# Converting attention weights to fp16 by DMA instead of by ScalarE, VectorE and GpSimd, and dealing VectorE's other steps one a unit

## Chip, cores, metric

The kernel runs on one core of one Trainium2 chip. The metric is the device time of one execution in microseconds (us).

## What is computed

Eight images of 512 channels and 32 x 32 = 1024 tokens go through two attention layers. The change is in the first layer:

```
h   = group_norm(x); qkv = qkv_w @ h + qkv_b          # 8 heads of 64 channels
q, k, v = fake_quant(q), fake_quant(k), fake_quant(v) # 8 bits, one scale for the whole tensor
w   = softmax(q^T k / sqrt(64)) over the keys
a   = v w^T
x   = x + proj_w @ a + proj_b
```

The second layer is group norm, single-head attention over all 512 channels, a projection and the residual, image by image.

## The kernel before

**Stages.** First, q, k and v of all images are computed and stored in DRAM with their minima and maxima, since the quantizing scales need the whole tensor. Then the first layer's attention runs for all images (`attention`, a generator). Image 0's attention runs alone, beside a weight folding for the second layer (`fold`, L208 `fold` matmuls), which one `next(folding)` per odd unit deals out to TensorE. From image 1 on, the attention of an image runs between the second-layer blocks of the image before.

**Units.** The attention's unit is (image b, pair of heads j, half hf of the queries, key tile s): 8 images x 4 pairs x 2 halves x 8 key tiles = 512 units, 64 of them in image 0. A unit does, in this order:

- `scores`: two `st` matmuls (one for each head of the pair), then ScalarE's exponential from PSUM into `pt` (128 x 1024, fp32). `pt` comes from a ring of four buffers.
- `split`: `pt` is turned into two fp16 parts, `two`: a high part (a cast) and a low part (`pt` minus the high part, a subtraction on VectorE, the inner function `rest`). `two` comes from a ring of six.
- `over_keys`: eight `av` matmuls with the quantized v (four column quarters, two parts).
- `totals`: four `sm` matmuls with ones, for the softmax's sums.

In image 0 the units with `plain(b, s)`, that is s = 3 and 7, aren't split. Their `pt` lies in a separate ring of three (`aside`), and `av` and `sm` are fp32 matmuls on it, with an fp32 copy of v (`vfs`, written by `whole`). Of image 0's other units, s = 2 and 6 are cast by GpSimd, s = 5 by VectorE, and s = 0, 1 and 4 by ScalarE.

**Order.** A step of the main loop handles four units: `st` runs six to eight units ahead of `av`; `need(u - 4)` makes sure that the subtraction of unit u - 4 has been written before the exponential of unit u. After the last unit of a pair, `finish` copies `av` and `sm` out of PSUM by ScalarE, sends the sums through DRAM to be spread (`apart`, `rs_d`, then `rs`, which comes back as a broadcast), and VectorE divides (`divide`, writing `ao`). At the first unit of a pair `load_pair` fetches the next pair's q, k and v into `raw` buffers (two of them, on SP's DMA queue), and VectorE quantizes them in two steps each (`quant`, `quant2`).

From image 1's third loop step on, the class `InOrder` plans the order on VectorE and ScalarE by hand with costs and due times (`later`, `fill`, `settle`; `InOrder.planned` is true). In image 0's attention and the first eight units of image 1 it isn't: `later` does its work at once, and the framework's scheduler orders the engines' instructions, with the written order as a priority. Nearly all of VectorE's and ScalarE's instructions carry the helper's line L91, all matmuls L208; tiles tell them apart.

Of the kernel before, what the change touches and what calls it, by code (L numbers as in the profile page):

```python
# [9 lines left out]
F32 = mybir.dt.float32  # L10
# [8 lines left out]
P = 128  # L19
# [3 lines left out]
NT = T // P  # L23
NH = T // 512
HEADS = 8
PAIRS = HEADS // 2
# [32 lines left out]
def attn_pair_kernel(  # L59
# [9 lines left out]
    nc = tc.nc  # L69
# [236 lines left out]
    with ExitStack() as fast:  # L306
# [39 lines left out]
        cut, at = {}, 0  # L346
# [526 lines left out]
        def quant2(raw, dst, i):  # L873
            dve.tensor_scalar(dst, raw, bhi[:, i : i + 1], MAGIC, ALU.min, ALU.subtract)
# [35 lines left out]
        vfs = {}  # L910

        def plain(b, s):
            return b == 0 and s % 4 == 3

        ao = {}

        def load_pair(b, j):

            nm = f"{b}_{j}"
            raws = []  # L920

# [12 lines left out]
            def whole(raw, _, i):  # L934
                quant2(raw.rearrange("p (t d) -> p t d", t=NT)[:, 3::4, :], vfs[j], i)

            fetch(0, q_d[b][j])
            fetch(1, k_d[b][j])
            qt = qkp.tile([P, T], BF, tag="q", name=f"q_{nm}")
            kt = qkp.tile([P, T], BF, tag="k", name=f"k_{nm}")  # L940
            vt = qkp.tile([P, NT, P], F16, tag="v", name=f"v_{nm}")
            todo = (qt, kt, vt.rearrange("p t d -> p (t d)"))

            if b == 0:
                vfs[j] = xp.tile([P, 2, 256], F32, tag="x", name=f"vf_{nm}")[:, :, 0:P]

            def quants(i):
                for step in (quant, quant2, *([whole] if i == 2 and b == 0 else [])):
                    dve.later(
                        "qk" if i < 2 else "qv", 0.7, lambda step=step: step(raws[i], todo[i], i),  # L950
                        pe.t + 12.0, 45.0,
                    )

            def fetch_v():
                if len(raws) == 2:
                    fetch(2, v_d[b][:, :, bass.ts(j, P)])
                quants(2)

            if (b, j) == (0, 0):
                fetch(2, v_d[b][:, :, bass.ts(j, P)])  # L960
            quants(0)
            quants(1)
            dve.later("qk", 0.0, fetch_v)
            return qt, kt, vt

        settle = dve.settle

        def attention():

# [4 lines left out]
                     for s in range(NT)]  # L974
            pairs = {}
            pairs[0, 0] = load_pair(0, 0)
            pts, parts, avs, sms, rss, ready = {}, {}, {}, {}, {}, {}
# [4 lines left out]
            def scores(u):  # L982
                b, j, hf, s = units[u]
                if hf == 0 and s == 0:
                    settle("qk")
                nm = f"{b}_{j}_{hf}"
                qt, kt, _ = pairs[b, j]
                st = pair_ps(f"st_{nm}_{s}")
                if b == 0 and u % 2 == 1:
                    next(folding, None)  # L990
                awaits(st_free[-2])
                for i, r in enumerate(HALF):
                    mm(
                        st[:, i, :], lhsT=kt[r, bass.ts(s, P)],
                        rhs=qt[r, bass.ts(hf, 512)], start=True, stop=True,
                    )
                if u >= 4:
                    need(u - 4)
                if plain(b, s):
                    pt = aside[:, u // 4 % 3].rearrange("p (i k) n -> p i (k n)", i=2)  # L1000
                else:
                    pt = ptp.tile([P, 2, 512], F32, tag="p", name=f"pt_{nm}_{s}")
                there = act.do(
                    1.12, lambda: act.activation(pt, st, AF.Exp, scale=esc),
                    max(pe.t + 0.25, ready.get(u - 4, 0.0) + 0.1),
                )
                st_free.append(there)
                pts[u] = pt, there

            def split(u):  # L1010

                b, j, hf, s = units[u]
                pt, there = pts.pop(u)
                if plain(b, s):
                    parts[u], ready[u] = pt, there
                    return
                two = partp.tile([P, 2, 2, 512], F16, tag="two", name=f"two_{b}_{j}_{hf}_{s}")
                parts[u] = two

                def rest():  # L1020
                    dve.tensor_tensor(two[:, 1], pt, two[:, 0], ALU.subtract)
                    ready[u] = dve.t

                def cast(copy=act.copy):
                    at_hand.add(u)
                    copy(two[:, 0], pt)  # L1026
                    done_at = act.t if copy == act.copy else there + 1.5
                    dve.later("sum", elements(1024), rest, done_at + 0.1, 9.0)

                if s % 4 == 2:  # L1030
                    cast(nc.gpsimd.tensor_copy)
                elif not InOrder.planned and s == 5:
                    cast(dve.tensor_copy)
                else:
                    act.later("cast", 1.02, cast, there, 7.0)

            def need(u):

                while u not in ready:
                    e, name = (act, "cast") if u not in at_hand else (dve, "sum")  # L1040
                    e.begin(next(i for i, c in enumerate(e.chores) if c[0] == name))

            def over_keys(us):
                need(us[-1])
                awaits(ready[us[-1]])
                pe.t += 0.12
                for u in us:
                    b, j, hf, s = units[u]
                    if s == 0:
                        avs[b, j, hf] = av_bank(f"av_{b}_{j}_{hf}")  # L1050
                    if plain(b, s):
                        for i in range(4):
                            r = slice(i * QUAD, (i + 1) * QUAD)
                            mm(
                                avs[b, j, hf][r, :], lhsT=vfs[j][:, s // 4, r],
                                rhs=parts[u][:, i // 2, :], start=False, stop=(s == NT - 1),
                            )
                        continue
                    for w in range(2):
                        for i in range(4):  # L1060
                            r = slice(i * QUAD, (i + 1) * QUAD)
                            mm(
                                avs[b, j, hf][r, :], lhsT=pairs[b, j][2][:, s, r],
                                rhs=parts[u][:, w, i // 2, :], start=(s == 0 and w == 0),
                                stop=(s == NT - 1 and w == 1),
                            )
# [17 lines left out]
            def finish(b, j, hf):  # L1084

                nm = f"{b}_{j}"
                if hf == 0:
# [35 lines left out]

            for u in (0, 2, 4):
                for i in (u, u + 1):
# [3 lines left out]
            for u in range(0, len(units), 4):  # L1129
                b, j, hf, s = units[u]  # L1130
                if hf == 0 and s == 0:
                    n = b * PAIRS + j + 1
                    if n < B * PAIRS:
                        pairs[divmod(n, PAIRS)] = load_pair(*divmod(n, PAIRS))
                    settle("qv")


# [28 lines left out]
                    two(split, u + 6)  # L1166
                    two(scores, u + 8)
                if s == NT - 4:
                    finish(b, j, hf)
# [993 lines left out]
```

## Time and profile before

| | |
|---|---|
| three runs, us | 2590.61, 2591.39, 2596.20 (median 2591.39) |
| the profiled execution, us | 2596.26, its span 2594.5 |
| busy share of the span | TensorE 98%, VectorE 73%, ScalarE 52%, GpSimd 7% |
| DMA | 243 MB, mean 94 GB/s |
| first `st` matmul of the attention | starts at 590.0 us |
| `aside` exponentials of image 0 | 16, the last starts at 703.1 us |
| first projection matmul of image 0 | starts at 726.0 us |

In the profile PE is TensorE's matmuls, PEld its weight loads, DVE VectorE, ACT ScalarE, POOL GpSimd, SP the queue that issues most DMAs. A group reads: line, engine, operation, output <- inputs, shapes, count | busy us, mean ns of one | idle us of the engine just before, with what released it. A busy TensorE isn't TensorE at its peak, as matmuls overlap at their ends. Two neighbouring `st` matmuls, one for each head, run beside each other.

### The profile page before, as it was taken

Reading aid. Unit: us, or ns where it says so; the run is one execution under the profiler, and the core shown is the slowest. Engines: PE = TensorE matmul, PEld = TensorE weight load, DVE = VectorE, ACT = ScalarE, POOL = GpSimd, SP = SyncE. Lnnn points to the kernel's source line nnn. Section 1 sums busy time; section 2 is a strip of 40 time slices with the busy share of each in tenths; the row PEclk is TensorE's granted clock in tenths of the full one; section 3 lists DMA queues with packets and bytes.
Section 4 is the critical chain, followed back from the end, with each engine's and each line's share of the span. In section 5 each row is a group of like instructions: output and inputs, shape, how many; then the busy total and the mean of one; then the engine's idle time right before and its main releaser. Section 6 shows DMA issues by size and latency. Waiting matters only on the chain.

```text
span 2594.5 us, 38713 instructions
## 1 busy us (share of the span) xinstructions
PE 2535.6 (98%) x15670; PEld 1754.2 (68%) x15670; DVE 1905.8 (73%) x2748; ACT 1360.4 (52%) x1696; POOL 193.8 (7%) x153
## 2 busy tenths in 40 slices
PE   7999999999989999999999999999999999999998
PEld 4788888873237765775677577757766775777687
DVE  6788777669867777777877787778777777775544
ACT  3222222218856674666566566647665765664121
POOL 0000000001110001000100011010001000100000
PEclk9899999999999999999999999999999999999999
DMA  4343333334311232223212332231232123212211
GB/s 167 130 148 139 115 119 118 129 126 135 115 50 54 58 111 102 66 78 111 87 56 70 125 99 58 94 107 63 85 107 98 46 79 122 83 51 84 86 37 38
DMA packets 156014, 243.09 MB, mean 94 GB/s; under 512 B 26545, under 2 KB 93105, under 8 KB 154289
## 3 DMA queue, kind: packets, MB, share of 16 engines
q1 hardware_dynamic: 125264, 182.81, 21.3%
q10 hardware_dynamic: 30560, 57.71, 6.5%
q8 instruction: 125, 2.05, 0.3%
q14 instruction: 65, 0.52, 0.1%
HBM read 153.64 MB, written 86.28 MB: 92 GB/s over the span
## 4 chain that ended last, share of the span: by engine, by line
PE 84%; DVE 5%; ACT 2%; issue 2%; DMA 2%; POOL 0%; SPq 0%; ACTq 0%; DVEq 0%
PE s L208 15%; PE o L208 14%; PE qkps L208 12%; PE pj L208 9%; PE av L208 7%; PE v2ps L208 7%; PE g L208 7%; PE vps L208 6%; PE st L208 4%; PE sm L208 3%; DVE two L91 2%; ACT pt L91 1%; DMA rs<-rs_d 0%; DVE acc L91 0%; DVE h L91 0%
## 5 line engine op out<-in xcount | busy, mean ns | idle before, releaser
L91 ACT ACTIVATE pt<-st,esc 128x1024 f32<-128x1024 f32 x496 | 528.6, 1115 | 348.7 <-PE st L208 326.2
L91 DVE TENSOR_TENSOR two<-pt,two 128x1024 f16<-128x1024 f32 x496 | 604.3, 1235 | 129.2 <-POOL two L1026 106.9
L91 ACT CAST two<-pt 128x1024 f16<-128x1024 f32 x358 | 362.6, 1056 | 5.3 <-ACT p L91 5.1
L1026 POOL CAST two<-pt 128x1024 f16<-128x1024 f32 x128 | 171.3, 1338 | 1537.3 <-ACT pt L91 771.5
L208 PE MATMUL av<-two,v 128*32 128x512 f16 x3968 | 244.7, 381 | 0.2
L208 PE MATMUL s<-g,h 128*128 128x256 f32 x1024 | 233.4, 380 | 0.0
L208 PE MATMUL pj<-ao,wp 128*128 128x512 f32 x512 | 223.8, 595 | 0.0
L208 PEld LDWEIGHTS s<-g,h 128*128 128x128 f32 x1024 | 192.9, 190 | 31.0 <-issue 4.3
L91 ACT ACTIVATE u_ring<-qkps,qkbt 128x512 f32<-128x512 f32 x89 | 61.1, 687 | 252.6 <-PE qkps L208 220.3
L208 PE MATMUL st<-q,k 64*128 64x512 bf16 x1024 | 165.8, 383 | 17.6 <-ACT pt L91 12.6
L208 PEld LDWEIGHTS <-v 128*32 128x32 f16 x3968 | 91.3, 96 | 134.0 <-issue 60.7
L208 PE MATMUL s<-g,sums 128*128 128x256 f32 x768 | 178.4, 381 | 0.2 <-DVE p L91 0.2
L208 PEld LDWEIGHTS pj<-ao,wp 128*128 128x128 f32 x512 | 96.0, 190 | 121.6 <-issue 111.1
L208 PE MATMUL o<-p,v 128*128 128x256 f32 x768 | 175.2, 382 | 1.0 <-DVE p L91 1.0
L208 PEld LDWEIGHTS o<-p,v 128*128 128x128 f32 x768 | 144.3, 190 | 27.1 <-issue 5.7
L208 PEld LDWEIGHTS s<-g,sums 128*128 128x128 f32 x768 | 144.7, 190 | 24.2 <-issue 4.1
L208 PEld LDWEIGHTS <-k 64*128 64x128 bf16 x1024 | 35.6, 94 | 156.6 <-issue 155.0
L208 PE MATMUL sm<-two,ones 128*32 128x512 f16 x1984 | 136.1, 379 | 1.9 <-ACT rs L91 1.9
L208 PE MATMUL qkps<-half,w_high 128*128 128x512 f32 x480 | 134.3, 402 | 0.0
L208 PE MATMUL qkps<-half,w_low 128*128 128x512 f32 x480 | 132.3, 398 | 1.9 <-DVE half L91 1.9
L208 PE MATMUL qkps<-half,w_mix 128*128 128x512 f32 x480 | 132.5, 398 | 0.6 <-DVE half L91 0.6
L208 PE MATMUL g<-h,wa 128*128 128x256 f32 x512 | 122.0, 387 | 2.7 <-DVE h L91 2.5
(219 smaller groups left out, 3838.3 us busy)
## 6 DMA issues: line engine op xcount, KB each, us to landing
rs<-rs_d SPq DMA_DIRECT2D x80, 256.0 KB
x<-in_x_dram SPq DMA_DIRECT2D x32, 512.0 KB
q_d<-wa SPq DMA_DIRECT2D x32, 512.0 KB
k_d<-wa SPq DMA_DIRECT2D x32, 512.0 KB
v_d<-v_ring SPq DMA_DIRECT2D x32, 512.0 KB
raw<-q_d SPq DMA_DIRECT2D x32, 512.0 KB
raw<-k_d SPq DMA_DIRECT2D x32, 512.0 KB
x_d<-h SPq DMA_DIRECT2D x64, 256.0 KB
```

Source lines behind the costliest of these rows:

```text
L91: ins = self.latest = op(*args, **kw).ins
L208: ins = nc.tensor.matmul(ps, lhsT=lhsT, rhs=rhs, **kw).ins
L1026: copy(two[:, 0], pt)
```

## The change

Image 0 keeps one fp32 unit in eight (s = 7). Of the other seven, s = 1, 2, 3, 5 and 6 get their high part by a casting DMA, `pt` (fp32) to `two` (fp16) in SBUF, issued from GpSimd's queue; s = 0 and 4 stay on ScalarE. The subtraction of a unit cast by DMA is put off: it is written when the unit two later is split, or when `need` asks for it. The branch by which VectorE casts s = 5 while nothing is planned is deleted, so in image 1's first units ScalarE casts that tile.

VectorE's other steps of the unplanned part (quantizing, the fetch of v, the reciprocal `spread`, `divide`) go into a list, `dealt`, each with the unit from which it may run: 10 units after the load for q, k and the fetch of v, 18 for v, 10 after `finish` for `spread` and 15 for `divide`. Each `split` then writes one of them at most; `settle(what)` writes all that are left of a kind where the program needs them.

```diff
         def plain(b, s):
-            return b == 0 and s % 4 == 3
+            return b == 0 and s % 8 == 7
+        dealt = []
+        def deal(u):
+            i = next((i for i, (at, *_) in enumerate(dealt) if at <= u), None)
+            if i is not None:
+                dealt.pop(i)[2]()
+        def settle(what):
+            while True:
+                i = next((i for i, (_, name, _) in enumerate(dealt) if name == what), None)
+                if i is None:
+                    break
+                dealt.pop(i)[2]()
+            dve.settle(what)
...
+        CAST_BY_DMA = (1, 2, 3, 5, 6)
-        def load_pair(b, j):
+        def load_pair(b, j, u=None):
...
             def whole(raw, _, i):
-                quant2(raw.rearrange("p (t d) -> p t d", t=NT)[:, 3::4, :], vfs[j], i)
+                quant2(raw.rearrange("p (t d) -> p t d", t=NT)[:, 7::8, :], vfs[j], i)
...
                 for step in (quant, quant2, *([whole] if i == 2 and b == 0 else [])):
-                    dve.later(
-                        "qk" if i < 2 else "qv", 0.7, lambda step=step: step(raws[i], todo[i], i),
-                        pe.t + 12.0, 45.0,
-                    )
+                    name, work = "qk" if i < 2 else "qv", lambda step=step: step(raws[i], todo[i], i)
+                    if u is None or InOrder.planned:
+                        dve.later(name, 0.7, work, pe.t + 12.0, 45.0)
+                    else:
+                        dealt.append((u + (10 if i < 2 else 18), name, work))
...
-            dve.later("qk", 0.0, fetch_v)
+            if u is None or InOrder.planned:
+                dve.later("qk", 0.0, fetch_v)
+            else:
+                dealt.append((u + 10, "qk", fetch_v))
...
             def split(u):
                 b, j, hf, s = units[u]
                 pt, there = pts.pop(u)
+                if not InOrder.planned:
+                    for v in [v for v in put_off if v < u - 1]:
+                        put_off.pop(v)()
+                    deal(u)
...
+                if b == 0 and s in CAST_BY_DMA:
+                    nc.gpsimd.dma_start(two[:, 0], pt)
+                    put_off[u] = rest
+                    return
...
                 if s % 4 == 2:
                     cast(nc.gpsimd.tensor_copy)
-                elif not InOrder.planned and s == 5:
-                    cast(dve.tensor_copy)
                 else:
                     act.later("cast", 1.02, cast, there, 7.0)
             def need(u):
+                if u in put_off:
+                    put_off.pop(u)()
...
-                    dve.later("ao", elements(1100), divide, dve.t + 7.0, 20.0)
-                dve.later("ao", 0.4, spread, pe.t + 5.0, 8.0)
+                    if InOrder.planned:
+                        dve.later("ao", elements(1100), divide, dve.t + 7.0, 20.0)
+                    else:
+                        dealt.append((u + 15, "ao", divide))
+                if InOrder.planned:
+                    dve.later("ao", 0.4, spread, pe.t + 5.0, 8.0)
+                else:
+                    dealt.append((u + 10, "ao", spread))
```

The indices of `aside` (`u // 8 % 3`) and of `vfs` (`s // 8`) follow, and `load_pair` and `finish` are given the unit's number.

More of the change, by code (lines that the diff above doesn't have):

```diff
@@ L944, in load_pair @@
             if b == 0:
-                vfs[j] = xp.tile([P, 2, 256], F32, tag="x", name=f"vf_{nm}")[:, :, 0:P]
+                vfs[j] = xp.tile([P, 2, 256], F32, tag="x", name=f"vf_{nm}")[:, 0:1, 0:P]
             def quants(i):
                 for step in (quant, quant2, *([whole] if i == 2 and b == 0 else [])):
-                    dve.later(
-                        "qk" if i < 2 else "qv", 0.7, lambda step=step: step(raws[i], todo[i], i),
-                        pe.t + 12.0, 45.0,
-                    )
+                    name, work = "qk" if i < 2 else "qv", lambda step=step: step(raws[i], todo[i], i)
[3 more added lines that the diff above has]
+                        dealt.append((u + (10 if i < 2 else 18), name, work))
             def fetch_v():
@@ L962, in load_pair @@
             quants(1)
-            dve.later("qk", 0.0, fetch_v)
+            if u is None or InOrder.planned:
+                dve.later("qk", 0.0, fetch_v)
+            else:
+                dealt.append((u + 10, "qk", fetch_v))
             return qt, kt, vt
-        settle = dve.settle
         def attention():
@@ L976, in attention @@
             pairs[0, 0] = load_pair(0, 0)
-            pts, parts, avs, sms, rss, ready = {}, {}, {}, {}, {}, {}
+            pts, parts, avs, sms, rss, ready, put_off = {}, {}, {}, {}, {}, {}, {}
             st_free, at_hand = [0.0, 0.0], set()
@@ L999, in scores @@
                 if plain(b, s):
-                    pt = aside[:, u // 4 % 3].rearrange("p (i k) n -> p i (k n)", i=2)
+                    pt = aside[:, u // 8 % 3].rearrange("p (i k) n -> p i (k n)", i=2)
                 else:
@@ L1054, in over_keys @@
                             mm(
-                                avs[b, j, hf][r, :], lhsT=vfs[j][:, s // 4, r],
+                                avs[b, j, hf][r, :], lhsT=vfs[j][:, s // 8, r],
                                 rhs=parts[u][:, i // 2, :], start=False, stop=(s == NT - 1),
@@ L1082, in totals, with finish @@
                                stop=(s == NT - 1 - (b == 0 and n > 1)))
-            def finish(b, j, hf):
+            def finish(b, j, hf, u):
                 nm = f"{b}_{j}"
@@ L1133, in attention @@
                     if n < B * PAIRS:
-                        pairs[divmod(n, PAIRS)] = load_pair(*divmod(n, PAIRS))
+                        pairs[divmod(n, PAIRS)] = load_pair(*divmod(n, PAIRS), u)
                     settle("qv")
@@ L1168, in attention @@
                 if s == NT - 4:
-                    finish(b, j, hf)
+                    finish(b, j, hf, u)
                 two(split, u + 8)
```

## The prediction

> **What bounds the kernel now.** I read the page first. Its chain of work puts 84% of the span on TensorE, so time can only be won where TensorE waits or by giving it less. The edit touches the first image's attention, so I found that stretch by the `st` matmuls: the first starts at 590 us, the exponential of unit 63, the image's last, starts at 703.15, and the projection begins at 726. Then I cut it in three with the busy time by stage (busy us, instructions in brackets):
>
> ```profile
> core 0: us, PE busy (x) PEld busy (x) DVE busy (x) ACT busy (x) POOL busy (x), PEclk, DMA share, GB/s
> 585.00:600.00 15.00, 12.33 (x33) 4.02 (x32) 12.25 (x25) 11.33 (x13) 1.91 (x1) 0.90 0.66 231
> 600.00:680.00 80.00, 80.00 (x676) 24.86 (x678) 73.05 (x86) 71.35 (x78) 15.84 (x11) 1.00 0.30 95
> 680.00:726.00 46.00, 36.15 (x406) 12.49 (x398) 39.63 (x43) 42.77 (x47) 10.51 (x7) 1.00 0.40 126
> ```
>
> Three limits stand side by side. From 600 to 680, while the weight folding gives TensorE extra matmuls, TensorE has no idle time at all. After 680 ScalarE is the fullest, 42.77 of 46. VectorE is at 73.05 of 80 and 39.63 of 46, close behind both. By the count of `st` matmuls (two a unit) 44 units start in the middle stretch, 80/44 = 1.82 us each. Over the image it is 113 us from the first `st` to the exponential of the last unit: 1.77 us each.
>
> TensorE's rows in the timeline give the price of a unit, from one start to the next:
>
> ```profile
> 622.46 0.39 PE L208 MATMUL st<-q,k 64*128 64x512 bf16 x2
> 622.77 1.05 PE L208 MATMUL av<-two,v 128*32 128x512 f16 x16
> 623.65 0.60 PE L208 MATMUL sm<-two,ones 128*32 128x512 f16 x8
> 624.18 0.39 PE L208 MATMUL st<-q,k 64*128 64x512 bf16 x2
> 624.50 1.13 PE L208 MATMUL fold<-wn_v 128*128 128x512 f32 x2
> 625.56 0.39 PE L208 MATMUL st<-q,k 64*128 64x512 bf16 x2
> 625.88 0.61 PE L208 MATMUL av<-two,v 128*32 128x512 f16 x8
> 626.32 1.03 PE L208 MATMUL av<-aside,vf 128*32 128x512 f32 x8
> 627.18 0.39 PE L208 MATMUL sm<-two,ones 128*32 128x512 f16 x4
> 627.40 1.03 PE L208 MATMUL sm<-aside,ones 128*32 128x512 f32 x4
> 628.36 0.39 PE L208 MATMUL st<-q,k 64*128 64x512 bf16 x2
> ```
>
> Two fp16 units take 0.88 us for `av` and 0.53 for `sm`: 0.44 + 0.265 = 0.705 each. One fp32 unit (`aside`) takes 626.32 to 627.18 and 627.40 to 628.36: 0.86 + 0.96 = 1.82. One unit made fp16 frees 1.115 us of TensorE.
>
> The groups of VectorE in 600 to 680, and the views of the tiles in 585 to 735 (min/median/max ns), show what GpSimd costs it:
>
> ```profile
> L91 DVE TENSOR_TENSOR two<-pt,two 128x1024 f16<-128x1024 f32 x34 | 47.0, 1410 | 0.1
> L91 DVE TENSOR_SCALAR raw<-raw,rcp 128x1024 f32<-128x1024 f32 x8 | 6.8, 848 | 4.3 <-DMA raw<-v_d 2.3 <-DMA raw<-k_d 1.4 <-DMA raw<-q_d 0.6
> L91 DVE TENSOR_TENSOR two<-pt,two x62: 1160/1218/2089, 596.0 to 731.1; 128x1024 f16<-128x1024 f32 x62
> L1026 POOL CAST two<-pt x19: 1037/1345/2451, 596.2 to 723.3; 128x1024 f16<-128x1024 f32 x19
> ```
>
> A subtraction is 1.21 us when alone, up to 2.09 beside a GpSimd cast; the cast itself stretches from 1.04 to 2.45. Finally the chain in order of time, for what a transfer takes here:
>
> ```profile
> 588.28 4.70 DMA raw<-q_d
> 648.88 5.73 DMA raw<-q_d
> 694.21 1.43 DMA rs_d<-rcs
> ```
>
> **The change, part by part.** The image has 64 units, 8 of which go from fp32 to fp16.
>
> *TensorE.* `av` runs six to eight units behind `st`, so in 600 to 680 it does the fp32 units 3, 7, ... 43; six of these eleven (3, 11, ... 43) become fp16. 6 x 1.115 = 6.7 us, all on the path as long as TensorE stays the fullest there: 80 becomes 73.3, or 1.67 us a unit.
>
> *VectorE, same stretch.* Six more subtractions, 6 x 1.21 = 7.3. Gone: six casts of 0.686 (4.1), the GpSimd surcharge on 34 subtractions, 34 x 0.20 = 6.8, and the like on the quantizing steps, 8 x 0.10 for `raw` and 3 x 0.26 for `v` (1.004 against 0.747 us alone) = 1.6. 73.05 becomes 67.8, under 73.3, so the added subtractions cost nothing while TensorE covers them; without that cover they would cost their 7.3. The quarter-size `vf` step halves its 0.35: nothing.
>
> *ScalarE, same stretch.* It casts s = 0, 1, 4 now, 0 and 4 after: about 5.5 x 1.05 = 5.8 less of 71.35. It doesn't bound there, so no gain.
>
> *Start.* ScalarE casts units 0 and 1 one after the other at 593, and an `st` then waits 2.13 us for ScalarE at 596. One of the casts goes: 1.1 us won.
>
> *Tail, 680 to 726.* ScalarE loses the cast of unit 57 and gets those of units 69 and 77 of the next image, which VectorE had (that branch is deleted for both images). One cast more on the fullest engine: 1.1 us lost.
>
> *The dealt work.* Loads, quantizing steps, the reciprocal with its three SP transfers, and the division are written 10 to 18 units later, one a unit. VectorE idles 4.3 us for `raw` and 2.3 for `rs` in the stretch; VectorE being covered, I count nothing for it. On SP's queue the `v` load moves behind the q and k steps, and the `rs` transfers move behind two subtractions or more; `rs` is asked for five units (9 us) after its spread, against 5.9 us in the chain (1.39 to `rs_d`, 0.52 of issue, 3.96 back), so it is hidden. The cover is thin: the written order is a priority and not the order on the engine (pair 2's first quantizing step runs at 601.8, long before its place), so the steps may also land elsewhere.
>
> *The DMA casts.* This is the unknown: no GpSimd queue transfer is in the trace. 40 are issued, each reads 512 KB and writes half. A cast that is late holds its subtraction at the head of VectorE's queue, with the next units' subtractions and the dealt steps behind it; on GpSimd only further casts are queued behind a waiting one. Who waits for VectorE is ScalarE, through the four `pt` buffers: the exponential of the fourth non-fp32 unit later waits for this unit's subtraction. With Lw the time from the exponential's end to the subtraction's start, a unit by DMA takes 1.12 + Lw + 1.21 round, one by ScalarE 1.12 + 1.05 + 1.21 and about 0.5 of queueing, 3.88. Seven such hops (five and two) span 32 units: T = (5 x (2.33 + Lw) + 7.76)/32 = 0.607 + 0.156 Lw. Bounds of Lw: below, the 8 KB transfer and one SP issue of 0.32, 1.43 + 0.32 = 1.75, T = 0.88; above, the slowest `raw` load, the slowest GpSimd cast for the work of issuing, and a whole subtraction ahead: 5.73 + 2.45 + 1.21 = 9.4, T = 2.07. I take the `raw` load at 588, nearest in bytes and rows, a GpSimd cast alone as a stand-in for issuing, and half a subtraction: 4.70 + 1.04 + 0.6 = 6.3, T = 1.59, under TensorE's 1.67. The two meet at Lw = 6.8, so there is half a microsecond to spare and no more. Bandwidth speaks against more: five reads of 0.52 MB each 13.4 us are 196 GB/s on top of 95 to 126.
>
> One rule speaks against the change. The Trainium skill, "SBUF — State Buffer", in "SBUF: two separate sides", says that a DMA issued from GpSimd has its descriptors written by GpSimd, which VectorE locks out for the length of a two-port operation; the trace shows the like for casts (1.04 against 2.45 us), for descriptors nothing. If each issue waited out one 0.75 us step, Lw would be 7.05, T 1.71, and 44 x 0.04 = 1.8 us of the gain would go. The other way, "DMA: Bandwidth & Descriptors", "Anatomy of one DMA — SWDGE (gpsimd) path", gives 2.0 us and bytes over 436 GB/s: an estimate of 3.2 us for these 512 KB, against the 4.70 of the row; by it the sum is the same and the margin 1.5 us wider.
>
> **Sum.** -6.7 - 1.1 + 1.1 = -6.7 us. The profiled execution took 2596.26 (span 2594.5) and would take 2589.6; it lies 4.9 above the median of the runs, so against 2591.39 I forecast 2584.7.
>
> **The rivals.**
> 1. *The DMA casts pace the image* (slower). The four `pt` buffers hold up the exponentials. For: 0.5 us of margin, and the `raw` loads already vary from 4.3 to 5.7 us. Against: the shares of the DMA engines are 0.30 and 0.40. It beats the present 1.77 us a unit from Lw = 7.45. At 8.5: T = 1.93, 64 x 1.93 = 123.7 against 113, +10.6: 2602. At the upper bound 9.4 +19.
> 2. *The gain is eaten* (no change). Lw near 7.2, or the dealing leaves VectorE's waits where they are beside new ones for DMAs: T about 1.73, 64 x 0.04 = 2.4 us won: 2589.
> 3. *More is won.* The start's TensorE idle goes wholly (15 - 12.33 = 2.7) and ScalarE's idle in the tail too (46 - 42.77 - 1.1 = 2.1): 6.7 + 2.7 + 2.1 = 11.5: 2580. For: VectorE is relieved everywhere. Against: 2.3 of ScalarE's 3.2 idle us in the tail are one wait for a division on VectorE, which the program still has in front of the same copy.
> 4. *The dealing does nothing* (the scheduler hoists the steps back): VectorE 67.8 + 6.6 = 74.4 over 73.3, 1.1 lost: 2585.8. Inside the forecast.
>
> **How the numbers follow.** 0.2% is 5.2 us, about what a measurement of this kernel can tell from no change; so faster means under 2586.2, slower over 2596.6. Forecast with rival 4: 0.40, of which 0.04 ends short of 5.2; rival 3: 0.14; rival 2: 0.14; rival 1: 0.32. Faster 0.50, same 0.18, slower 0.32. The range goes from rival 3's 2580, rounded out, to a little over rival 1's price; what lies beyond (Lw over 8.6, a gain over 12 us) I put at 0.15 to 0.2. The likeliest case alone is 2582 to 2588.
>
> **What would show it.** Right: in a stretch with folding TensorE still has no idle, eight `aside` exponentials are left, subtractions have a median and a mean near 1.21, `st` has a step of 1.67, and VectorE's waits for `raw` are gone. Wrong: ScalarE's exponentials wait for "DVE two", VectorE's subtractions wait for "DMA two", TensorE idles before 680; or a DMA cast is seen to take over 6 us from issue to landing, or GpSimd over 2 us to issue one.

## The result, and the profile after

| us | before | after |
|---|---|---|
| median (six runs each) | 2591.81 | 2612.66 |
| the profiled execution; its span | 2596.26; 2594.5 | 2610.88; 2609.1 |
| first `st`; last exponential of image 0; first `pj` | 590.0; 703.15; 726.0 | 588.1; 717.03; 744.2 |

The ratio is 1.0077 (95% interval 1.0066 to 1.0088): slower, and outside the predicted range. From the first `st` to the first projection matmul it now takes 156.1 us against 136.0; the start lies 1.9 us earlier, so `pj` comes 18.2 us later. The span of these two profiled executions is 14.6 us longer; between the medians it is 20.9.

TensorE's account of that stretch says what became of the gain. The busy time by stage, first of before, then of after, with the columns of the prediction's first fence (PE, PEld, DVE, ACT, POOL, clock, DMA share, GB/s):

```profile
590.00:726.00 136.00, 123.48 (x1099) 39.43 (x1098) 119.97 (x138) 124.07 (x134) 28.26 (x19) 0.99 0.35 113
```

```profile
588.10:744.20 156.10, 123.85 (x1099) 40.31 (x1098) 113.53 (x137) 118.38 (x128) 26.68 (x43) 0.92 0.68 162
```

The same number of matmuls; eight fp32 units fewer should have brought the busy time down by 8 x 1.115 = 8.9 us, to 114.6. It stayed at 123.85, at a granted clock of 0.92 for 0.99: by this sum about 9.3 us went to matmuls at a lower clock. (Every busy interval weighed by its granted clock gives 10.1 us lost in after and 1.7 in before, so 8.4 us more, and at full clock a saving of 8.2 in place of 8.9.) Idle time rose from 12.5 to 32.2 us. So -8.9 + 9.3 + 19.7 = +20.1. The DMA share doubled.

The three stages of the prediction, after:

```profile
core 0: us, PE busy (x) PEld busy (x) DVE busy (x) ACT busy (x) POOL busy (x), PEclk, DMA share, GB/s
585.00:600.00 15.00, 9.90 (x30) 3.13 (x29) 9.49 (x19) 9.48 (x10) 2.29 (x3) 1.00 0.76 221
600.00:680.00 80.00, 71.05 (x610) 23.01 (x609) 59.77 (x78) 59.99 (x64) 13.81 (x25) 0.94 0.77 177
680.00:726.00 46.00, 34.23 (x328) 11.07 (x327) 32.01 (x35) 31.40 (x36) 6.36 (x12) 0.85 0.71 168
```

No engine is full any more: TensorE 71 of 80, VectorE and ScalarE 60 each. Such a picture means that they wait for one another or for transfers. The waits of after in 588 to 735 us (us in total, times, longest) name the ring:

```profile
ACT pt L91 <- DVE two L91: 26.1, 12, 6.0
PE st L208 <- ACT pt L91: 23.5, 17, 4.2
DVE two L91 <- DMA two<-pt: 20.5, 14, 6.4
POOL two L1049 <- PE sm L208: 16.3, 5, 5.7
POOL two L1049 <- PE st L208: 15.1, 7, 3.8
DVE ao L91 <- DMA rs<-rs_d: 6.0, 3, 3.2
DVE raw L91 <- DMA raw<-q_d: 4.9, 2, 2.9
```

In before, in the same stretch, two of these rows were small, and the rows on casting DMAs were not there:

```profile
PE st L208 <- ACT pt L91: 8.5, 10, 2.1
ACT pt L91 <- DVE two L91: 1.6, 3, 0.7
```

A subtraction waits for a casting DMA, an exponential for the subtraction that must free its `pt` buffer, the `st` matmuls for the exponential. GpSimd in its turn waits for TensorE before it may issue a cast, since a `two` buffer must be free. In the view of the tile `two` (ns min/median/max for instructions):

```profile
L91 DVE TENSOR_TENSOR two<-pt,two x70: 1161/1219/2056, 593.5 to 748.5; 128x1024 f16<-128x1024 f32 x70
L1049 POOL DMA_DIRECT2D two<-pt x40: 527/530/1217, 591.7 to 721.2; - x40
DMA to landing us min/median/max: 2.9/4.0/9.5
```

GpSimd needs 0.53 us to issue, about half of the 1.04 that the prediction took as a stand-in; the subtractions run alone at 1.22, as forecast. From issue to landing it is 2.9 us at best and 9.5 at worst. One stall in the timeline of after (start, duration, engine; idle time before it in brackets):

```profile
621.94 1.03 ACT L91 CAST two<-pt 128x1024 f16<-128x1024 f32 x1
622.08 2.15 SPq L946 DMA_DIRECT2D raw<-q_d  x1
627.46 2.36 DVE L91 TENSOR_TENSOR two<-pt,two 128x1024 f16<-128x1024 f32 x2 [4.00 <-DMA two<-pt]
628.77 2.27 ACT L91 ACTIVATE pt<-st,esc 128x1024 f32<-128x1024 f32 x2 [4.78 <-DVE two L91]
629.94 0.39 PE L208 MATMUL st<-q,k 64*128 64x512 bf16 x2 [3.16 <-ACT pt L91]
630.18 0.53 POOL L1049 DMA_DIRECT2D two<-pt  x1 [5.36 <-ACT pt L91]
```

A `v` load, a `q` load and an `x` load are issued from 617 to 624 beside the casts; the DMA engines' share in 620 to 630 is 1.04. VectorE stands for 4.00 us on one cast, with the subtraction of the unit that ScalarE cast at 621.94 behind it; ScalarE stands 4.78, TensorE 3.16, GpSimd 5.36. At 692.4 it happens once more, beside the folding's `wm_d` stores, for 6.44 us.

What an idle TensorE costs besides is seen in slices of 2.5 us of after:

```profile
597.50:600.00 2.50, 0.00 (x0) 0.00 (x0) 1.88 (x3) 0.00 (x0) 0.00 (x0) 1.00 0.97 283
600.00:602.50 2.50, 1.25 (x10) 0.40 (x13) 2.01 (x4) 1.11 (x1) 0.53 (x1) 0.59 0.75 146
602.50:605.00 2.50, 2.50 (x22) 0.60 (x14) 2.50 (x4) 2.12 (x2) 0.32 (x1) 0.50 0.92 223
605.00:607.50 2.50, 2.50 (x10) 0.65 (x12) 1.27 (x2) 2.16 (x2) 0.64 (x1) 0.54 0.82 160
607.50:610.00 2.50, 2.50 (x30) 0.90 (x28) 2.29 (x2) 1.82 (x2) 0.53 (x1) 1.00 0.04 6
```

After an idle time that ended in a wait of 3.81 us the clock is 0.50 to 0.59 in the three slices from 600 to 607.5. The Trainium skill, "TensorE: Matmul & The Clock Gate", Part 1, states that the array falls to half its clock after an idle window of about 3.4 us and gets it back after a busy one. The trace agrees in the half. It shows besides that no single long pause is needed: two waits of 0.64 and 1.06 us left TensorE busy for half of 3.41 us, and the next 3.41 us, all of them busy, ran at 0.50.

```profile
682.36:685.77 3.41, 1.71 (x16) 0.60 (x11) 3.41 (x4) 2.65 (x4) 0.53 (x1) 1.00 0.19 36
685.77:689.18 3.41, 3.41 (x24) 0.90 (x26) 3.41 (x6) 3.41 (x5) 0.00 (x0) 0.50 0.69 160
```

### The profile page after: what moved, and what is told of

Read it like the earlier page. It is cut to its first block, busy times and chain, and to the rows that moved or that the text cites. A ratio compares the mean times of both kernels' runs of the same rounds, so it can differ in the third digit from the quotient of the medians.

```text
span 2609.1 us, 38823 instructions
## 1 busy us (share of the span) xinstructions
PE 2530.2 (97%) x15670; PEld 1751.1 (67%) x15670; DVE 1899.7 (73%) x2746; ACT 1355.6 (52%) x1690; POOL 191.7 (7%) x177
## 4 chain that ended last, share of the span: by engine, by line
PE 82%; DVE 5%; DMA 4%; ACT 2%; issue 2%; POOL 0%; SPq 0%; ACTq 0%; DVEq 0%; POOLq 0%
PE s L208 15%; PE o L208 13%; PE qkps L208 12%; PE pj L208 9%; PE av L208 7%; PE v2ps L208 7%; PE vps L208 6%; PE g L208 6%; PE st L208 4%; PE sm L208 3%; ACT pt L91 1%; DVE two L91 1%; DMA two<-pt 1%; DVE h L91 1%; DMA out_dram<-x 1%
## 5 line engine op out<-in xcount | busy, mean ns | idle before, releaser
L91 ACT ACTIVATE pt<-st,esc 128x1024 f32<-128x1024 f32 x504 | 537.1, 1115 | 374.2 <-PE st L208 328.6
L91 ACT CAST two<-pt 128x1024 f16<-128x1024 f32 x352 | 356.6, 1056 | 5.3 <-ACT p L91 5.1
L1055 POOL CAST two<-pt 128x1024 f16<-128x1024 f32 x112 | 146.8, 1311 | 1439.8 <-PE sm L208 764.4
L208 PE MATMUL av<-two,v 128*32 128x512 f16 x4032 | 251.4, 384 | 1.1 <-ACT ao L91 0.8
L208 PE MATMUL g<-h,wa 128*128 128x256 f32 x512 | 120.9, 384 | 2.2 <-DVE h L91 2.1
```

Of the source, the lines that this page charges most:

```text
L91: ins = self.latest = op(*args, **kw).ins
L208: ins = nc.tensor.matmul(ps, lhsT=lhsT, rhs=rhs, **kw).ins
```

## The experiments

In the table, T is the time of a unit: from the first exponential to the 64th, over 63. Busy and idle are TensorE's, from the first `st` to the first `pj`, in the profiled run; with one fp32 unit in eight and full clock about 114.6 us would be busy, with two 123.5. "5 MB moved" puts the folding's first loads and stores (`wp`, `x` and `wm_d`) behind image 0; most of those runs pay for it at the end of image 0 (in e3, e5 and e16 `pj` stops for 8.8 to 8.9 us after its first matmuls, until the last division is done; in e3 that division's reciprocals take 12.2 us to reach DRAM beside the moved transfers), so they are read by T and not by their total. T of one kernel seems to scatter by about 0.02: before has 1.778, and two kernels that turned out to equal it in time, e8 and e18, 1.800 and 1.758.

| run | ratio to before, 95% | T | busy | idle |
|---|---|---|---|---|
| before | 1 | 1.778 | 123.5 | 12.5 |
| after | 1.0077 (1.0066 to 1.0088) | 2.027 | 123.9 | 32.2 |
| e1 no DMA casts | 1.0036 (1.0024 to 1.0049) | 1.900 | 120.5 | 24.5 |
| e2 nothing dealt | 1.0079 (1.0057 to 1.0101) | 2.031 | 125.8 | 31.1 |
| e3 5 MB moved | 1.0097 (1.0077 to 1.0117) | 1.907 | 122.9 | 26.2 |
| e4 deeper exponentials | 1.0063 (1.0045 to 1.0080) | 1.960 | 122.8 | 31.8 |
| e5 e3 and e4 | 1.0084 (1.0059 to 1.0108) | 1.861 | 122.0 | 25.4 |
| e6 fewer fp32 units alone | 1.0027 (1.0017 to 1.0037) | 1.888 | 122.2 | 24.5 |
| e7 before, s = 2, 6 by DMA | 1.0034 (1.0024 to 1.0044) | 1.943 | 130.0 | 18.2 |
| e8 before, dealt | 0.9996 (0.9986 to 1.0006) | 1.800 | 124.9 | 13.4 |
| e9 after, written order held | 1.0058 (1.0035 to 1.0081) | 1.969 | 123.0 | 28.9 |
| e10 before, dealt, order held | 1.0025 (1.0016 to 1.0035) | 1.791 | 125.6 | 15.4 |
| e11 e7, 5 MB moved | 1.0015 (1.0005 to 1.0025) | 1.783 | 123.9 | 13.2 |
| e12 e5, order held | 1.0080 (1.0057 to 1.0102) | 1.875 | 120.9 | 26.2 |
| e13 e5, more pair buffers | 1.0084 (1.0058 to 1.0110) | 1.890 | 120.8 | 29.7 |
| e14 two casts by DMA | 1.0031 (1.0020 to 1.0041) | 1.854 | 120.5 | 25.3 |
| e15 e14, deeper exponentials | 1.0002 (0.9992 to 1.0012) | 1.761 | 118.9 | 20.4 |
| e16 e15, more pair buffers, 5 MB moved | 1.0052 (1.0035 to 1.0069) | 1.775 | 120.5 | 20.2 |
| e17 e14, second buffer for sums | 1.0016 (1.0007 to 1.0025) | 1.820 | 117.0 | 23.9 |
| e18 before, second buffer for sums | 1.0001 (0.9990 to 1.0012) | 1.758 | 126.3 | 11.3 |

### The parts of the change, one by one

e1, the changed kernel without casts by DMA:

```diff
-        CAST_BY_DMA = (1, 2, 3, 5, 6)
+        CAST_BY_DMA = ()
...
-                if s % 4 == 2:
+                if s % 4 == 2 or b == 0 and s == 3:
                     cast(nc.gpsimd.tensor_copy)
+                elif not InOrder.planned and s == 5:
+                    cast(dve.tensor_copy)
```

> The changed kernel with no casting DMA: one key tile of eight still in fp32 and VectorE's steps still dealt, but s = 2, 3 and 6 are cast by GpSimd, s = 5 by VectorE, s = 1 with 0 and 4 by ScalarE. The stretch from the attention's first st to the first projection matmul is 136.0 us before and 156.1 after. Theory A (the casts land late when other transfers fill the DMA engines): without them the loss is gone, and the 6.7 us that TensorE saves show: stretch 129 to 137, time 2585 to 2593. Theory B (the dealt and put-off order on VectorE is what costs, whoever casts): the stretch stays above 148, time above 2603.

2602.69 us, between what both had expected: the casts by DMA cost about half of the loss, and something else the rest. e6 narrows it down: the same kernel with nothing dealt either, so that only the eight fewer fp32 units are left of the change (the high part of these, s = 3, is cast by GpSimd).

> One fp32 unit in eight, no casting DMA (s = 2, 3, 6 by GpSimd, 5 by VectorE, 0, 1, 4 by ScalarE) and nothing dealt. With dealing this took 1.90 us a unit and 2602.7 us. If dealing is neutral, since the scheduler orders the steps anyway: 1.87 to 1.93 and 2600 to 2605: the loss is then VectorE's, which has eight subtractions more beside more GpSimd casts. If dealing costs: 1.78 to 1.84 and 2590 to 2597.

2601.15 us. The busy time by stage of e6:

```profile
600.00:680.00 80.00, 70.52 (x620) 24.50 (x624) 74.44 (x86) 64.27 (x71) 19.92 (x16) 1.00 0.30 94
```

TensorE has lost its idle-free stretch and VectorE is the fullest, 74.44 of 80 for some 42 units (80/1.888): 1.76 us a unit, against TensorE's 1.67. The exponentials' wait for the ring of four is there as well, without any cast by DMA (588 to 725 us; 1.6 us in before):

```profile
ACT pt L91 <- DVE two L91: 15.7, 6, 3.6
```

A unit that is no longer fp32 brings VectorE a subtraction, and it leaves the spare ring of three for the ring of four, which now serves seven units of eight in place of six. Giving TensorE less to do adds waits by both ways. How much each costs is not shown: no run gave e6 the deeper ring of e4. In after the casts by DMA do take work from VectorE (59.77 in 80 us for 39 units, 1.52 a unit), but bring their own waits.

e2 takes the dealing out of the change, e8 puts it alone into the kernel before. The edit of e2, in part:

```diff
-                    if InOrder.planned:
-                        dve.later("ao", elements(1100), divide, dve.t + 7.0, 20.0)
-                    else:
-                        dealt.append((u + 15, "ao", divide))
...
+                    dve.later("ao", elements(1100), divide, dve.t + 7.0, 20.0)
...
-                        pairs[divmod(n, PAIRS)] = load_pair(*divmod(n, PAIRS), u)
+                        pairs[divmod(n, PAIRS)] = load_pair(*divmod(n, PAIRS))
```

(`spread` likewise. Without `u`, `load_pair` hands its steps on at once.)

> The changed kernel with VectorE's other steps written at once, as before, in place of dealt; the casting DMAs stay. Theory A: the stretch stays at 152 to 160 us, time 2607 to 2616. Theory B: the stretch falls to 136 to 142, time 2591 to 2598.

> The kernel before with VectorE's other steps dealt and nothing else. If the scheduler undoes the dealing: 1.76 to 1.80 us a unit, 2589 to 2594. If dealing does what it says, VectorE's 9.4 us of waits for raw and 5.0 for rs shrink under 5 together, and 2 to 4 us are won: 2587 to 2590. If it costs: over 2596.

Without the dealing the change takes 2614.02 us (2612.66 with it); the dealing alone is 0.9996 (0.9986 to 1.0006) of before: no effect is seen either way. The order that the scheduler makes passes over the written one, as it did before: in e8 VectorE still waits 8.6 us for `raw` and 4.5 for `rs`. e9 and e10 hold VectorE to the written order, by making every one of its instructions depend on the one written before:

```diff
                     tc.add_manual_dep(ins, self.last.name, IN_ORDER, reason="order")
+                    if self.strict and name != "dma_start":
+                        self.last = ins
...
+            dve.strict = True
```

> The changed kernel with VectorE's instructions of image 0 held to the order in which they are written, so that the dealing and the put-off subtractions take effect instead of being a priority that the scheduler may pass over. VectorE waited 20.5 us for casts, 12.7 for raw and 6.0 for rs. If these waits at the head of VectorE's queue come from the order: raw and rs together under 6, casts under 14, from 2.03 to 1.80-1.92 us a unit, time 2595 to 2605. If the casts are too late in whatever order: 1.97 or more, over 2608.

> The kernel before with VectorE's steps dealt and held to the written order, no casting DMA and two fp32 units in eight. VectorE's 14.4 us of waits for raw and rs fall under 4. TensorE has no idle time from 600 to 680 and sets 1.78 us a unit, so at most the tail and the start gain: 1.72 to 1.78, 2586 to 2592. If the written order is worse than the scheduler's: over 1.82, over 2595.

With it the waits for `raw` are gone in e9, but others come: 10.4 us of VectorE for the row sums from DRAM (`rcs <- DMA apart`), 10.4 of TensorE for `k`, 7.1 of VectorE for ScalarE's casts. e10 is slower than before, so there the scheduler's order is the better one; e9 cannot be told from after (1.0058, 1.0035 to 1.0081, beside 1.0077). In neither kernel does the written order win time.

### The casts by DMA

e7 leaves the kernel before as it is, but casts s = 2 and 6 by DMA in place of GpSimd:

```diff
+        CAST_BY_DMA = (2, 6)
...
+                if b == 0 and s in CAST_BY_DMA:
+                    nc.gpsimd.dma_start(two[:, 0], pt)
+                    put_off[u] = rest
+                    return
```

> The kernel before, but s = 2 and 6 of image 0 are cast by DMA in place of GpSimd, with the subtraction put off; two fp32 units in eight as before, nothing dealt. If a casting DMA costs only where it is on the ring of buffers and where the DMA engines are full: six of eight units share four buffers, a turn takes about 1.12 + 4.2 + 1.21 = 6.5 us over 5.33 units = 1.22, far under 1.78, and VectorE sheds about 8 us of GpSimd's interference: 1.72 to 1.79 a unit, 2586 to 2593. If a late cast at the head of VectorE's queue costs in itself: 1.82 to 1.90, 2595 to 2603.

Sixteen such casts alone cost 12.6 us at `pj` (738.6 for 726.0). e11 is the same with the 5 MB moved behind image 0:

```diff
-                    load_wp(0, nc.sync.dma_start)
-                    load_x2(0, nc.sync.dma_start)
...
-            for t, dst in zip(wm, wm_d):
-                nc.sync.dma_start(dst, t)
+            stores.extend(zip(wm_d, wm))
...
         for _ in folding:
             pass
...
+        load_wp(0, behind)
+        load_x2(0, behind)
+        for dst, src in stores:
+            behind(dst, src)
```

> Two casting DMAs in eight units and nothing else (1.94 us a unit, VectorE waiting 12.3 us in 5 places for a cast), with the 5 MB of other transfers moved behind image 0. If those waits are meetings with other transfers: under 5 us of them, 1.78 to 1.84 a unit. If a cast is late on quiet engines too: 1.90 or more. The time is 2595 to 2608 either way, since the moved transfers hold up the projection.

T goes from 1.943 back to 1.783 and `pj` to 725.8. The waits, of e7 and then of e11, in 588 to 725 us:

```profile
DVE two L91 <- DMA two<-pt: 12.3, 5, 4.1
ACT pt L91 <- DVE two L91: 9.1, 6, 3.0
```

```profile
DVE two L91 <- DMA two<-pt: 1.5, 2, 1.4
ACT pt L91 <- DVE two L91: 2.7, 3, 1.5
```

Landings are 2.8/3.6/8.6 us in e7 and 2.8/3.4/6.0 in e11: the median hardly moves, the longest does. With two casts by DMA in a kernel that TensorE paces, nearly the whole loss of T goes with the meetings of a cast and another large transfer. (No run moved the 5 MB in a kernel without casts by DMA, so what that alone does to T is not shown; in before TensorE has no idle time from 600 to 680 with the 5 MB in their place.)

e3 is that edit on the changed kernel, e4 a deeper ring of exponentials, e5 both:

```diff
-                if plain(b, s):
-                    pt = aside[:, u // 8 % 3].rearrange("p (i k) n -> p i (k n)", i=2)
+                if b == 0 and s in (3, 6, 7):
+                    pt = aside[:, (3, 6, 7).index(s)].rearrange("p (i k) n -> p i (k n)", i=2)
```

> The changed kernel with 5 MB of other transfers (the second layer's weight and input, 3 MB loaded at 617 us, and the four folded weights stored, 2 MB at 656 to 693) moved behind the last sums of image 0; the casting DMAs stay. Theory A: VectorE's waits of 4.0 us at 623 and of 6.4 us at their places and the slower clock after them go; from the first st to the last fp32 exponential 128.9 us become 114 to 120, the stretch 140 to 147 (the moved loads then hold up the projection by up to 5), time 2595 to 2604. Theory B, and a theory C in which every cast is too slow even on quiet DMA engines: 126 to 130 and 154 to 160, time over 2609.

> The changed kernel with more buffers for the exponentials: the fp32 unit uses one of the three buffers of aside, and the units s = 3 and 6 use the other two, so five units of eight share the four pt buffers. Theory A with the ring of buffers as the way in which a late cast stops ScalarE: ScalarE's 26.1 us of waits for the subtraction fall under 12, the stretch to 140 to 148, time 2595 to 2604. If VectorE's order is what holds ScalarE, not the number of buffers: waits stay over 20, stretch over 152, time over 2607.

> The changed kernel with both the 5 MB of other transfers moved behind image 0 and the deeper set of buffers (units s = 3 and 6 in the spare buffers of aside). A unit of image 0 takes 1.78 us before, 2.03 after, 1.91 with the transfers moved and 1.96 with the buffers alone. If late casts and the four buffers together make the loss: 1.66 to 1.76 a unit, near the 1.67 that TensorE needs while folding. If what is left is VectorE's order (each subtraction stands behind others that wait): 1.84 to 1.92. The time itself is 2597 to 2612 either way, since the moved transfers hold up the projection by some 8 us.

T falls from 2.027 to 1.907 with less traffic, to 1.960 with a deeper ring, to 1.861 with both. The waits of e5 in 588 to 725 us:

```profile
DVE two L91 <- DMA two<-pt: 4.9, 5, 3.2
DVE two L91 <- DMA two<-aside: 3.5, 3, 2.2
ACT pt L91 <- DVE two L91: 3.6, 3, 1.9
PE av L208 <- DVE two L91: 8.7, 10, 1.6
```

The waits of the ring that the profile of after named are down to 8.4 and 3.6 us (18.3 and 26.1 in the same stretch there), and still TensorE idles 25.4 us. e12 held e5 to the written order, and e13 gave it two more pair buffers, because GpSimd's waits for TensorE were still long in e5 (21.4 and 15.1 us):

> The changed kernel with all three: the 5 MB moved, the deeper set of buffers, VectorE held to the written order. If meetings, buffers and order are the whole loss: 1.66 to 1.74 us a unit. If not, 1.80 or more and a cause is missing. The time is 2590 to 2606, with the projection held up by the moved transfers.

```diff
-                two = partp.tile([P, 2, 2, 512], F16, tag="two", name=f"two_{b}_{j}_{hf}_{s}")
+                if b == 0 and s in (1, 5):
+                    two = spare[:, s // 4]
+                else:
+                    two = partp.tile([P, 2, 2, 512], F16, tag="two", name=f"two_{b}_{j}_{hf}_{s}")
```

> The changed kernel with the 5 MB moved behind image 0 and the exponentials of s = 3 and 6 in spare buffers (as in the run that had both), and now also the fp16 pairs of s = 1 and 5 in two buffers of their own, so that the ring of six `two` buffers serves five units in eight instead of seven. In the run without this, GpSimd waited 36.5 us (11 times) for TensorE's row sums or scores before it issued a cast, and a unit took 1.862 us against 1.907 with four buffers for exponentials. Theory A, the pair buffers hold the casts back: those waits fall below 12 us and a unit takes 1.70 to 1.78 us. Theory B, what is left are the raw tiles' quantizing steps and the reciprocals' round trip through DRAM, at which VectorE and ScalarE stand: the GpSimd waits may go, but a unit stays within 0.03 of 1.862 us and `ao <- rs` and `raw` still show over 18 us together. In both the end is held by the moved transfers, so the total stays at 1.005 to 1.009.

e12 stayed at 1.875, with 10.3 us of TensorE waiting for `k` among the new waits. In e13 GpSimd's waits for TensorE are gone, VectorE's for casts are 1.3 us in all, and T is 1.890. What stands out in its waits (588 to 712 us) is the end of a pair:

```profile
ACT rs L91 <- DVE ao L91: 12.1, 2, 7.7
DVE ao L91 <- DMA rs<-rs_d: 11.4, 2, 6.9
PE sm L208 <- ACT rs L91: 8.6, 2, 6.4
```

So the pair buffers did not hold the pace. The row sums' way through DRAM comes late here as well: 11.4 us of waits, 4.2 in before. Whether the casts by DMA delay it is not shown; in after, with as many of them, it is 6.0.

### Fewer casts by DMA

e14 keeps the change, but casts only s = 3 and 5 by DMA (GpSimd 2 and 6, ScalarE 0, 1 and 4, VectorE none); e15 adds the deeper ring, e16 also the pair buffers and the 5 MB moved.

```diff
-        CAST_BY_DMA = (1, 2, 3, 5, 6)
+        CAST_BY_DMA = (3, 5)
```

> The changed kernel, but only s = 3 and 5 of eight cast by DMA; s = 2 and 6 are cast by GpSimd itself as before, 0, 1 and 4 by ScalarE, 7 is fp32. VectorE casts nothing. Theory A, the loss grows with the casts that go through the DMA queues and with the subtractions queued behind them: a unit takes 1.80 to 1.88 us (2.03 with five casts by DMA, 1.90 with none), the total 1.000 to 1.003. Theory B, any late cast stalls the in-order engines about as much: a unit takes 1.92 us or more, the total 1.004 or more, as when two casts by DMA were put into the kernel before (1.943, 1.0034).

> The same with two casts by DMA, and the exponentials of s = 3 and 6 in spare buffers. Theory A, the ring of four exponentials is what passes a late cast on to TensorE: a unit falls by 0.05 us or more below the run with four buffers, to 1.74 to 1.83 us, and the total comes to 0.998 to 1.001. Theory B, VectorE's order passes it on: within 0.03 us of the run with four buffers.

> The same with two casts by DMA, spare buffers for exponentials (s = 3, 6) and for pairs (s = 1, 5), and the 5 MB moved behind image 0. If late casts, through rings and collisions, are the whole cause, TensorE's own 1.67 us per unit comes through: 1.67 to 1.75 us, image 0's last fp32 exponential before 699; the moved transfers then hold the end, total 1.000 to 1.004. If something else of the change costs time (one more subtraction in eight on VectorE, the half clock after idle stretches, the pair's end), a unit stays at 1.78 us or more.

Five casts by DMA cost more than two (T 2.027, then 1.854), though none at all is no better (1.900 in e1), and the ring comes on top of it (1.761): e15 equals before, 1.0002 (0.9992 to 1.0012). It is the best form of the change that was run, and does not beat the kernel before. e16 lessens all the causes found so far at once and gives no more, 1.775, where TensorE's own work is 1.67.

TensorE's waits in e16, 591 to 708 us:

```profile
PE sm L208 <- ACT rs L91: 6.8, 2, 4.1
PE st L208 <- ACT pt L91: 5.2, 6, 2.1
PE st L208 <- ACT aside L91: 1.6, 3, 0.6
```

e17 gives the row sums of every other pair a buffer of their own in e14 (with s = 3 and 7 in spare buffers), so that ScalarE's copy need not wait for the division; e18 does that in the kernel before.

```diff
-                    rss[b, j] = l1p.tile([P, NH, 512], F32, tag="rs", name=f"rs_{nm}")
+                    if b == 0 and j % 2:
+                        rss[b, j] = aside[:, 2].rearrange("p (h k) n -> p h (k n)", h=NH)
+                    else:
+                        rss[b, j] = l1p.tile([P, NH, 512], F32, tag="rs", name=f"rs_{nm}")
```

> The kernel with two casts by DMA (s = 3, 5) and spare buffers for exponentials, now for s = 3 and 7 alone; the third spare buffer holds the row sums of pairs 1 and 3, so that ScalarE's copy of the next pair's sums does not wait for the division of the pair before. With one buffer, VectorE stood 4.7 us at `ao <- rs`, ScalarE 7.8 us at `rs <- ao`, TensorE 6.1 us at `sm <- rs`, and a unit took 1.760 us. Theory A, once casts are no longer late it is this chain at the pairs' ends that keeps TensorE from its 1.67 us: TensorE's `sm <- ACT rs` falls below 2 us, a unit takes 1.66 to 1.73 us, and the total comes to 0.996 to 0.999. Theory B, the chain only covers another wait of the same length (scores for ScalarE, VectorE's share of 92%): a unit stays within 0.03 us of 1.760 and the total at 0.999 to 1.002.

> The kernel before with the same second buffer for the row sums (its fp32 exponentials rotate through two spare buffers instead of three). There TensorE waited 1.9 us at `sm <- rs` and had nearly no idle time in 600 to 680 us. Theory A: nothing to win where TensorE is itself the pace, 0.9990 to 1.0010, 1.76 to 1.79 us per unit. Theory B, the chain costs the kernel before as well: 0.998 or less.

The waits of e17 in 591 to 703 us:

```profile
PE st L208 <- ACT pt L91: 7.1, 8, 2.1
ACT pt L91 <- DVE two L91: 5.8, 6, 1.6
PE av L208 <- DVE two L91: 5.3, 5, 2.3
```

`sm <- rs` has left TensorE's list (6.1 us in e15), and others stand in its place; s = 6 went back to the ring of four for it, which may be a part of them. T is 1.820. e18 is no different from before. No single wait was found that holds back the gain.

## Why the prediction was wrong

**The ring's hop for ScalarE's casts failed first.** The prediction wrote T = (5 x (2.33 + Lw) + 7.76)/32 and chose Lw well: from an exponential's end to its subtraction's start the trace of after has 6.07 us on average over all 56 units, about 6.4 for those cast by DMA, against the 6.3 taken. But "one by ScalarE 1.12 + 1.05 + 1.21 and about 0.5 of queueing, 3.88" leaves out what the prediction itself had said two sentences earlier: the next units' subtractions stand behind a late one. For s = 0 and 4 that time was about 5.2 us and not 1.55, so their hop is about 7.5. Then T = (5 x 8.77 + 2 x 7.49)/32 = 1.84, over TensorE's 1.67 and over the 1.78 of before, with Lw as it was taken. The trace of before gave a sign: there the same time was already 4.20 us on average over its 48 split units and 4.55 for s = 0 and 4, with no transfer in it. With 4.55 the prediction's sum comes to 1.78, no gain. (A part of it was free in before, since a buffer then stood empty for 2.6 us on average until its next exponential.)

**The rest of 2.03 is bursts and the clock.** The formula goes by a mean. The stalls of 4.00 and 6.44 us come where casts meet `raw`, `x` and `wm_d` transfers; e3 and e11 show that such meetings cost time. The prediction held the mean DMA share of 0.30 to 0.40 against this rival; the change itself raised it to 0.77, and slices reach 1.04. That TensorE's matmuls run at half the clock after such stalls was not in the sum at all: 8 to 9 us of the stretch's 20.1.

**"So the added subtractions cost nothing while TensorE covers them" held for VectorE's load and failed for the change.** Its load fell as said: 67.8 us for 44 units are 1.54 a unit, measured 1.52. But the cover was a sum of busy times. It needs VectorE busy for 92% of the time (67.8 of 73.3), and in after, with its waits for casts, it was busy for 75% (59.77 of 80). Where the casts stayed on the engines it did reach 93%, and then it was the fullest engine itself (e6).

**TensorE's -6.7.** Busy time does fall where the clock holds: 117.0 in e17 against 123.5 in before, both at a clock of 0.99. That is 6.6 us for eight units, where 1.115 each would be 8.9, so the price of a unit was taken somewhat high. It is no gain of time: idle time takes its place in every run, in e15 and e16 as well (20 us for 12.5), where few casts are late. In e16 no one wait of TensorE's has more than 6.8 of these 20 us; whether VectorE's share (71.0 of 80), the end of a pair or the rings in alternation keep the gain away stays open.

**The start** (-1.1) did not come: TensorE is busy 9.90 of the first 15 us instead of 12.33, with the 3.81 us wait there. The first `st` lies between 584.5 and 590.4 in the profiles of all these kernels, so the 1.9 us cannot be put down to the change. **The tail** (+1.1) is buried in the stretch's loss.

**The dealt work** at nothing: right, by e2 and e8, and for the reason of rival 4.

**The rivals.** Rival 1, casts by DMA pace the image, was the right mechanism with the right signs in the profile (all three that were named). Its price of 10.6 us was too small: it is 18.2 at `pj` and 20.9 in the medians, by its upper bound of 19, which the range had left out. That the bound comes near is luck, for it stood on Lw = 9.4, and Lw was 6.4. **GpSimd's issuing**, the rule that spoke against the change, shows in no issue: one takes 0.53 us, 1.22 at most in after and 1.30 in any run (e4). Whether writing the descriptors held up a landing is not told apart here. **The landing**: the Trainium skill, "DMA: Bandwidth & Descriptors", section "Anatomy of one DMA — SWDGE (gpsimd) path", gave an estimate of 3.2 us for these 512 KB; the trace has 2.9 at best, 4.0 in the median, 9.5 at worst. For the path it is the longest that count: from e7 to e11 the median hardly moves.

## What to carry to other kernels

When a step is moved to a slower but otherwise idle resource, work out the ring with the delay of the in-order engine behind it applied to every unit that passes that engine, not only to those that were moved. Look up the worst slice of a shared resource, after adding what the change itself puts there, rather than its mean. A saving on the fullest engine is worth little when the next one is nearly as full: here VectorE stood at 91% (73.05 of 80), and no run turned TensorE's saving into time. Idle time that lowers TensorE's clock is paid for again in the matmuls after it.

## What the hardware showed that was not expected

A casting DMA of 512 KB to 256 KB from GpSimd's queue lands 2.8 to 2.9 us after issue at the earliest in every kernel here, and takes 1.43 us of all 16 DMA engines: the queue has 2.2% of 2609.1 us for 40 of them.

```profile
q0 software_dynamic: 5760, 10.49, 2.2%
```

TensorE's clock drops to half in the middle of a kernel after waits of three to four microseconds, and after shorter ones that add up to half of 3.41 us (682 to 686 us of after). `av` on one fp32 unit took 1.45 us at 630.7, right after the stall that was shown, instead of 1.03:

```profile
630.70 1.45 PE L208 MATMUL av<-aside,vf 128*32 128x512 f32 x8
```
